# A gated-delta-rule recurrence: substitution in one piece ahead of the keys' taps, keys by row on ScalarE, two projections tied behind the feed-forward

## The chip, the core and the metric

The kernel runs on one core of a Trainium2 chip. The core has TensorE (PE in the profile, its weight loads PEld), VectorE (DVE), ScalarE (ACT), GpSimd (POOL) and SyncE (SP), which here only issues DMAs. Each engine has its own queue of instructions, worked through in order; they wait for each other through semaphores. The metric is the device time of one execution in microseconds (us), the median of the runs shown.

## The reference, cut to what matters

Two transformer layers over 2 sequences of 1024 tokens with 256 features, layernorm after every block, all in float32: attention with 32 heads of 8 (8 key heads), a feed-forward with silu gate and int8 weights, a gated delta rule with 16 heads of 128, and a feed-forward with signs as weights. The change lies in the third block:

```python
q = _silu(_dwconv_causal(x @ Wq, conv_q_w, conv_q_b))      # k and v likewise; 4 taps
alpha = _sigmoid(x @ Wa + ba); beta = _sigmoid(x @ Wb + bb)
def step(S, inp):                                          # over the tokens, one by one
    qt, kt, vt, at, bt = inp
    err = einsum('bhvk,bhk->bhv', S, kt) - vt
    S = at * S - bt * err[..., None] * kt[:, :, None, :]
    o = einsum('bhvk,bhk->bhv', S, qt)
    return (S, o)
o = layernorm(o) * ln_w + ln_b
out = (o * sigmoid(x @ Wg)) @ Wo
```

## The kernel before, in words

The first layer (attention in two passes, then its feed-forward) takes the time up to about 820 us. Its feed-forward is a generator (`before` in `delta_rule`, L147), so that the first steps of the delta rule run beside it.

The delta rule works in **steps** `i` = 0 to 31: four halves of 512 tokens (two for each sequence) times 8 slots of two heads (L37, L38). One step takes two heads through 512 tokens in four chunks of 128. A chunk is solved as a block (`recur`, L590): pr = v + M k (L618, L622), copied to prs on ACT (L625); pw = inverse times prs (L633), copied to wc on ACT (L636); pm = keys by row times wc (L645), from which DVE makes the next state M (L650, L652); po = output (L659, L660), copied on ACT (L663). Each needs the one before.

Around `recur` stand the helpers of other steps, which fill PE between these matmuls:

- `keys(i+4)` (L283) projects the keys (L891 to L893, three matmuls for each of two halves of the 256 features), convolves them (`conv`, L258), makes the decays `at` with a scan on DVE (L306), the triangle `lt` of keys against keys (L315, L316), and stores its 32x32 diagonal blocks to DRAM (L328). `conv` is one evacuation on ACT (L265), three taps on DVE (L272) under `tc.high_priority()`, in the second half of a sequence the ends carried over from the first (L278), and a silu on ACT (L279). For the first slot of such a half, `carry` (L249) computes these ends on POOL, with a scratch tile `part` that shares the tag "tmp", and so the two buffers, with the substitution's scratch tile `tmp`.
- `blocks(i)` (L338), once for two steps, inverts 16x16 triangles by forward substitution. It loads the stored blocks into `ll` (L345), copies the identity into a PSUM bank on ACT (L355), and does 15 times a product and a difference on DVE (L360, L363; 128x15 to 128x64 elements). Then ACT copies the result to `tt` (L365), one DMA stores it (L367), eight load it in another arrangement as `dt` (L373), and DVE transposes it into `dd` (L376).
- `levels(i)` (L379), once for two steps, builds the inverse of the whole 128x128 triangle from these blocks in several rounds of small matmuls. Its first (L387, 128 matmuls) reads `dd`, its second (L397) `n0` made on DVE (L389), and DVE transposes a second time (L401).
- `others(i+1)` (L494): projections of v and q (`pair`, L446), `key_rows` (L452: four transposes of the keys on PE, L458, then one DVE instruction over 128x512 that scales them by the last decay of their chunk, L460), the gate's projection (L483), `scores` (L465, L470, L471), `decayed` (L477).
- `finish` (L528) normalizes the outputs (o on POOL, DVE and ACT, L555, L558), transposes them (L564), applies the gate (ACT L567, DVE L568), and projects them (L891 to L893 with tile pf).

The **order of the work** has three sources. `Places` (L95) writes the helpers' pieces out by hand: a step has 120 units, each `yield` names the unit of the next piece (AT_BLOCKS = 44 and 52 and then 2.2 units for each substitution step, AT_LEVELS from 43 of the next step, AT_KEYS = 91). From step 0 on, `InLine.link` (L133) ties every matmul to the one written before it (`te.strict`, L772), so that PE's order is the written one. On the other engines a planner that simulates the time puts the ready instruction with the best priority next; priority is the order of writing, and `tc.high_priority()` moves an instruction ahead of all normal ones. `after(a, b)` (L895) ties the order of two instructions without a wait across engines.

Where the feed-forward ends: at i = -2 it is drained (L776), and the first `blocks` and `others(0)` are written; at i = -1 come `keys(3)`, the first `levels`, the opening of the late pools (L780), whose memory is that of the feed-forward, and `rest_of_first` (L516), which holds the decays of step 0 and the projections of v and q for step 1. PE's order is not yet written here. At i = 0 come `recur(0)` and `gate_of_first` (L523), whose weights wg lie in the late pools.

Of the kernel before, what the change touches and what calls it, by code (L numbers as in the profile page):

```python
# [11 lines left out]
F32 = mybir.dt.float32  # L12
# [3 lines left out]
AF = mybir.ActivationFunctionType  # L16
ALU = mybir.AluOpType
# [3 lines left out]
P = 128  # L21
# [9 lines left out]
SCALE = DK ** -0.5  # L31
# [3 lines left out]
HC = HT // P  # L35
Q = 4
BL = P // Q  # L37
SB = BL // 2  # L38
U = HP * HC
# [104 lines left out]
def delta_rule(  # L144
# [13 lines left out]
    nc = tc.nc  # L158
# [3 lines left out]
    early = open_pool(left, "dearly", "left", 2)  # L162
# [24 lines left out]
    def q4(t):  # L187
        return t.rearrange("p (c t) -> p c t", t=P)
# [12 lines left out]
    dt = cst.tile([P, 2 * U, BL], F32, name="dt", tag="dt")  # L201
    nc.gpsimd.memset(lo, 0.0)
    nc.gpsimd.memset(dt, 0.0)
    ib = load(a["c_ib"], [P, BL], "ib")
# [23 lines left out]

    st = [dict() for _ in range(B * 2 * NS)]
    state, lines, copied = [None] * NS, Places(te), []  # L230
    last = B * 2 * NS - 1

    def place(i):
# [24 lines left out]
    def conv(m, i, h, bufs, pp):  # L258

        hi, s = place(i)  # L260
        n, hd = "qkv".index(m), s * HP + h
        acc = half_tile(early if m == "k" else conv_pool, m, bufs)

        with tc.high_priority():
            nc.scalar.activation(  # L265
                acc, pp, AF.Identity, bias=cb[:, n, hd : hd + 1], scale=cw[:, n, hd, KS - 1 : KS]
            )
            if hi % 2 == 0:
                nc.scalar.copy(halos[:, n, hd, :], pp[:, HT - KS + 1 :])

            for d in range(1, KS):
                made = nc.vector.scalar_tensor_tensor(  # L272
                    acc[:, d:], pp[:, 0 : HT - d], cw[:, n, hd, KS - 1 - d : KS - d], acc[:, d:], ALU.mult, ALU.add
                )
        if hi % 2:
            if s == 0 and h == 0:
                carry(n)
            nc.vector.tensor_add(acc[:, 0 : KS - 1], acc[:, 0 : KS - 1], ends[:, n, hd, :])  # L278
        nc.scalar.activation(acc, acc, AF.Silu)  # L279
        st[i][m, h] = acc  # L280
        return made

    def keys(i, t0):  # L283

        hi, s = place(i)
        col = halves[hi]["col"]
        pps = [project("k", i, h) for h in range(HP)]
        if i < last:
            st[i + 1]["wk"] = weights("k", place(i + 1)[1])
        for h in range(HP):  # L290
            taps = conv("k", i, h, 10, pps[h])
        yield t0 + AT_DECAY - AT_KEYS
        lt = early.tile([P, U, P], F32, name="lt", tag="lt", bufs=5)
        st[i]["lt"] = lt
        nc.gpsimd.memset(lt[:, :, 0:1], 0.0)
        for h in range(HP):
            hd = s * HP + h
            dec = decay(hi, hd, 0, "da")
            d1 = early.tile([P, HC, P], F32, name="d1", tag="raw", bufs=RAW)
            nc.gpsimd.affine_select(  # L300
                d1, col[:, :, hd].unsqueeze(2).to_broadcast([P, HC, P]),
                pattern=[[0, HC], [1, P]], compare_op=ALU.is_equal, fill=0.0, base=0, channel_multiplier=-1,
            )
            e = half_tile(early, "at", 10)
            after(
                nc.vector.tensor_tensor_scan(e, dec, d1.rearrange("p c t -> p (c t)"), 0.0, ALU.mult, ALU.add), taps  # L306
            )
            st[i]["at", h] = e
        for h in range(HP):
            yield t0 + AT_TRIANGLE[h] - AT_KEYS  # L310
            e, k = st[i]["at", h], st[i]["k", h]
            pkk = bank(ps_m, "m", "pkk")
            for c in range(HC):
                t = slice(c * P, (c + 1) * P)
                te.link(nc.tensor.matmul(pkk[:, t], lhsT=k[:, t], rhs=k[:, t], start=True, stop=True))  # L315
            nc.vector.scalar_tensor_tensor(  # L316
                lt[:, h * HC : (h + 1) * HC, 1:P], q4(pkk)[:, :, 1:P], SCALE, q4(e)[:, :, 0 : P - 1],
                ALU.mult, ALU.mult,
            )
        yield t0 + AT_TRIANGLE[2] - AT_KEYS  # L320
        n = i % 2
        if n == 0:
            st[i]["d1"] = dram.tile([Q, 2 * U, BL, BL], F32, name="d1_", tag="d1_")
        else:
            st[i]["d1"] = st[i - 1]["d1"]
        for q in range(Q):
            r = slice(q * BL, (q + 1) * BL)
            nc.sync.dma_start(  # L328
                out=st[i]["d1"][q, n * U : (n + 1) * U].rearrange("u j t -> j u t"), in_=lt[r, :, r]
            )  # L330
# [7 lines left out]
    def blocks(i, psum):  # L338

        NB = Q * 2 * U  # L340
        ll, tt, dd = split_block(i)
        d1 = st[i]["d1"]
        for h in range(2):
            r = slice(h * SB, (h + 1) * SB)
            nc.sync.dma_start(  # L345
                out=ll[h * NB : (h + 1) * NB], in_=d1.rearrange("q u j t -> (q u) j t")[:, r, r]
            )
        nc.sync.dma_start(out=tt.rearrange("p c r -> p (c r)"), in_=a["c_idl"])
        for q in range(Q):
            nc.sync.dma_start(  # L350
                out=lo[q * BL : q * BL + SB, :, SB:BL], in_=d1[q, :, 0:SB, SB:BL].rearrange("u j t -> j u t")
            )
        yield AT_BLOCKS[1]
        wide = bank(*psum, "pi")[:, 0 : SB * SB].rearrange("p (c r) -> p c r", r=SB)
        nc.scalar.copy(wide, tt)  # L355
        for j in range(SB - 1):
            n, m = j + 1, SB - 1 - j
            tmp = early.tile([P, 64], F32, name="tmp", tag="tmp")
            tm = tmp[:, 0 : n * m].rearrange("p (c r) -> p c r", r=m)
            nc.vector.tensor_mul(  # L360
                tm, wide[:, 0:n, j : j + 1].to_broadcast([P, n, m]), ll[:, j : j + 1, j + 1 : SB].to_broadcast([P, n, m])
            )
            nc.vector.tensor_sub(wide[:, 0:n, j + 1 : SB], wide[:, 0:n, j + 1 : SB], tm)  # L363
            yield AT_BLOCKS[1] + BLOCK_STEP * (j + 1)
        nc.scalar.copy(tt, wide)  # L365
        d2_ = dram.tile([2, Q, 2 * U, SB, SB], F32, name="d2_", tag="d2_")
        nc.sync.dma_start(  # L367
            out=d2_.rearrange("h q u c r -> (h q u) (c r)"), in_=tt.rearrange("p c r -> p (c r)")
        )
        for q in range(Q):  # L370
            for h in range(2):
                o = q * BL + h * SB
                nc.sync.dma_start(  # L373
                    out=dt[o : o + SB, :, h * SB : (h + 1) * SB], in_=d2_[h, q].rearrange("u c r -> c u r")
                )
        nc.vector.transpose(dd, dt.rearrange("p u t -> p (u t)"))  # L376
        st[i]["dd"] = dd.rearrange("p (u t) -> p u t", t=BL)

    def levels(i, psum):  # L379

        dd = st[i]["dd"]
        quarter = [slice(q * BL, (q + 1) * BL) for q in range(Q)]
        p0 = bank(*psum, "p0").rearrange("p (u t) -> p u t", t=BL)
        with tc.high_priority():
# [1 line left out]
                for r in quarter:  # L386
                    te.link(nc.tensor.matmul(p0[r, v, :], lhsT=lo[r, v, :], rhs=dd[r, v, :], start=True, stop=True))  # L387
        n0 = early.tile([P, 2 * U, BL], F32, name="n0", tag="tt", bufs=1)
        nc.vector.scalar_tensor_tensor(  # L389
            n0, p0, -1.0, ib.unsqueeze(1).to_broadcast([P, 2 * U, BL]), ALU.mult, ALU.add  # L390
        )
        yield AT_LEVELS[1]
        px = bank(*psum, "px").rearrange("p (u t) -> p u t", t=BL)
        with tc.high_priority():
# [3 lines left out]
        nc.scalar.copy(X[0 : 3 * BL, :, 0:BL], px[0 : 3 * BL])  # L398
        nc.scalar.copy(X[quarter[1], :, BL : 2 * BL], px[quarter[1]])

        nc.vector.transpose(dd.rearrange("p u t -> p (u t)"), px.rearrange("p u t -> p (u t)"))  # L401
        for n in range(2):
            for r in quarter:
                (nc.gpsimd.tensor_copy if n else nc.scalar.copy)(
# [46 lines left out]

    def key_rows(i, h):  # L452

        k, e = st[i]["k", h], st[i]["at", h]
        pk = bank(ps_m, "m", "pk")
        for c in range(HC):
            t = slice(c * P, (c + 1) * P)
            te.link(nc.tensor.transpose(pk[:, t], k[:, t], ident))  # L458
        kc = conv_pool.tile([P, HC, P], F32, name="kc", tag="kc", bufs=4)
        nc.vector.scalar_tensor_tensor(  # L460
            kc, q4(pk), -SCALE, q4(e)[:, :, P - 1 : P].to_broadcast([P, HC, P]), ALU.mult, ALU.mult
        )
        st[i]["kc", h] = kc

    def scores(i, h):  # L465
# [11 lines left out]
    def decayed(i, h):  # L477

        q, k, gs = st[i]["q", h], st[i]["k", h], st[i]["dg"][h]
        nc.gpsimd.tensor_mul(q4(k)[:, :, 1:P], q4(k)[:, :, 1:P], q4(gs)[:, :, 0 : P - 1])  # L480
        nc.gpsimd.tensor_mul(q, q, gs)
# [34 lines left out]
    def rest_of_first():  # L516
        decays(0)
        for h in range(HP):
            decayed(0, h)
        for m in "vq":  # L520
            pair(m, 1)

# [244 lines left out]
    def drain(g):  # L767
        for _ in g:
            pass

    for i in range(-AHEAD, last + 1):
        te.strict = i >= 0  # L772
        t = i * UNIT
        if i == -2:
            drain(blocks(0, (ps_m, "m")))
            drain(before)  # L776
        if i == -1:
            drain(keys(3, 0))
            drain(levels(0, (ps_m, "m")))
            open_late()  # L780
# [770 lines left out]
```

## Time and profile before

| | us |
|---|---|
| median of 3 runs | 2143.49 (2139.96 to 2144.91) |
| the profiled execution | 2145.29 |
| its span, first to last instruction | 2143.6 |
| PE busy in the span | 1916.0 (89%) |
| DVE busy | 1598.0 (75%) |
| ACT busy | 1111.1 (52%) |
| POOL busy | 789.0 (37%) |
| mean granted TensorE clock | 0.962 |

Lines of the profile are read so: in a list of groups, "L460 DVE SCALAR_TENSOR_TENSOR kc<-pk,at 128x512 x64" is line 460, run on DVE, writing tile kc from pk and at, 64 times, followed by the busy us, the mean ns of one, and the idle time of the engine just before them with what ended it. In a list of waits, "PE p L387 <- DVE ll L376: 16.6, 8, 5.1" says that PE stood 16.6 us in all ahead of L387, 8 times, at most 5.1 us, until DVE's instruction of L376 had ended. Where a wait is for several things, the list names the last event it saw. In a timeline each line has start, length, engine, line, operation, tiles and shape, a count of merged neighbours, and in brackets the idle time before it. The tile `ll` holds the blocks, the solution `tt` and the transposed `dd`; the tile p stands for p0 to p4, and pi for the PSUM bank `wide` of the substitution.

### The profile page before, as it was taken

Reading aid. Unit: us, or ns where it says so; the run is one execution under the profiler, and the core shown is the slowest. Engines: PE = TensorE matmul, PEld = TensorE weight load, DVE = VectorE, ACT = ScalarE, POOL = GpSimd, SP = SyncE. Lnnn points to the kernel's source line nnn. Section 1 sums busy time; section 2 is a strip of 40 time slices with the busy share of each in tenths; the row PEclk is TensorE's granted clock in tenths of the full one; section 3 lists DMA queues with packets and bytes.
Section 4 is the critical chain, followed back from the end, with each engine's and each line's share of the span. In section 5 each row is a group of like instructions: output and inputs, shape, how many; then the busy total and the mean of one; then the engine's idle time right before and its main releaser. Section 6 shows DMA issues by size and latency. Waiting matters only on the chain.

```text
span 2143.6 us, 48759 instructions
## 1 busy us (share of the span) xinstructions
PE 1916.0 (89%) x18656; PEld 1518.2 (71%) x18656; DVE 1598.0 (75%) x3886; ACT 1111.1 (52%) x2285; POOL 789.0 (37%) x1273
## 2 busy tenths in 40 slices
PE   4889999999987886989999899998988998988896
PEld 2455555555555886878888788887878887877775
DVE  6756666877748984888779778778777878866676
ACT  2365566576753453554544555554555554554442
POOL 1343332422122333444454344444344444334330
PEclk8999999999999998999999999999999999999997
DMA  7544443432033323434334434344433434433010
GB/s 222 162 149 139 141 142 119 156 103 78 34 81 108 92 65 89 122 102 122 97 106 119 121 108 117 104 124 113 128 102 98 138 89 122 117 103 91 20 46 20
DMA packets 313514, 230.91 MB, mean 108 GB/s; under 512 B 139648, under 2 KB 278656, under 8 KB 313280
## 3 DMA queue, kind: packets, MB, share of 16 engines
q1 hardware_dynamic: 299472, 210.80, 33.9%
q10 hardware_dynamic: 9632, 10.76, 1.5%
q0 software_dynamic: 4176, 6.23, 1.2%
q8 instruction: 147, 2.41, 0.5%
q14 instruction: 87, 0.71, 0.1%
HBM read 172.95 MB, written 51.87 MB: 105 GB/s over the span
## 4 chain that ended last, share of the span: by engine, by line
PE 53%; DVE 19%; DMA 6%; ACT 3%; SPq 3%; issue 3%; POOL 1%; POOLq 0%; ACTq 0%; DVEq 0%
PE av L1232 4%; PE ps L1211 4%; PE pp L891 4%; PE pp L893 4%; PE pp L892 4%; DVE k L272 3%; PE ps L1159 3%; DVE q L272 3%; PE pkq L470 3%; PE pm L645 2%; DVE v L272 2%; PE pr L622 2%; PE po L660 2%; SPq L373 2%; PE po L659 2%
## 5 line engine op out<-in xcount | busy, mean ns | idle before, releaser
L1168 DVE TENSOR_REDUCE mx<-ps 128x4 f32<-128x1024 f32 (+1 forms) x320 | 344.3, 1112 | 131.7 <-PE ps L1159 91.5
L1215 ACT ACTIVATE es<-ps 128x512 f32<-128x512 f32 (+1 forms) x608 | 315.2, 578 | 133.6 <-PE ps L1211 125.3
L1211 PE MATMUL ps<-qT,kT 128*128 128x512 f32 (+3 forms) x768 | 220.7, 369 | 17.6 <-ACT es L1215 15.5
L1159 PE MATMUL ps<-kT,qT 128*128 128x512 f32 x576 | 201.3, 424 | 20.9 <-DVE mx L1168 15.9
L1211 PEld LDWEIGHTS ps<-qT,kT 128*128 128x128 f32 x768 | 131.3, 190 | 104.9 <-ACT es L1215 53.7
L272 DVE SCALAR_TENSOR_TENSOR k<-pp,cw,k 128x511 f32<-128x511 f32 (+2 forms) x192 | 138.7, 741 | 45.1 <-ACT k L265 24.2
L272 DVE SCALAR_TENSOR_TENSOR q<-pp,cw,q 128x511 f32<-128x511 f32 (+2 forms) x192 | 138.9, 740 | 33.9 <-ACT q L265 16.4
L1232 PE MATMUL av<-es,vaug 128*32 128x512 f32 (+3 forms) x1536 | 162.6, 502 | 0.0
L1159 PEld LDWEIGHTS ps<-kT,qT 128*128 128x128 f32 x576 | 101.5, 191 | 82.1 <-DVE mx L1168 49.0
L272 DVE SCALAR_TENSOR_TENSOR v<-pp,cw,v 128x511 f32<-128x511 f32 (+2 forms) x192 | 138.2, 740 | 11.1 <-ACT v L265 7.1
L571 POOL CAST yh<-y 128x512 fp32r<-128x512 f32 x62 | 38.0, 613 | 271.4 <-DVE y L568 237.4
L841 POOL TENSOR_TENSOR wfl<-wf,wfh 128x256 fp32r<-128x256 f32 x80 | 58.6, 736 | 207.9 <-ACT wfh L929 181.3
L1218 POOL TENSOR_SCALAR_AFFINE_SELECT es<-es 128x512 f32<-128x512 f32 x128 | 80.7, 639 | 146.4 <-ACT es L1215 146.1
L300 POOL TENSOR_SCALAR_AFFINE_SELECT d<-col 128x512 f32<-128x512 f32 x64 | 59.9, 954 | 143.9 <-DVE at L306 126.9
L480 POOL TENSOR_TENSOR k<-k,dg 128x508 f32<-128x508 f32 x64 | 81.3, 1271 | 76.8 <-PE pkq L470 55.9
L625 ACT COPY prs<-pr 128x256 f32<-128x256 f32 x128 | 47.6, 372 | 114.7 <-PE pr L622 95.7
L660 PE MATMUL po<-wc,at 128*128 128x128 f32 x512 | 100.4, 285 | 0.0
L663 ACT COPY o<-po 128x256 f32<-128x256 f32 x128 | 47.5, 371 | 100.5 <-PE po L660 99.9
L659 PE MATMUL po<-M,q 128*128 128x128 f32 x448 | 90.8, 286 | 0.0
L622 PE MATMUL pr<-M,k 128*128 128x128 f32 x448 | 81.2, 276 | 8.4 <-DVE M L650 5.9
L633 PEld LDWEIGHTS pw<-prs,lt 128*128 128x128 f32 x512 | 78.3, 194 | 13.4 <-ACT prs L625 2.1
L1232 PEld LDWEIGHTS av<-es,vaug 128*32 128x32 f32 x1536 | 39.2, 110 | 67.7 <-issue 53.0
(309 smaller groups left out, 5600.9 us busy)
## 6 DMA issues: line engine op xcount, KB each, us to landing
wk<-w1k SPq DMA_DIRECT2D x64, 256.0 KB
da<-dec SPq DMA_DIRECT2D x64, 256.0 KB
wv<-w1v SPq DMA_DIRECT2D x64, 256.0 KB
wq<-w1q SPq DMA_DIRECT2D x64, 256.0 KB
dg<-dec SPq DMA_DIRECT2D x64, 256.0 KB
wg<-w1g SPq DMA_DIRECT2D x64, 256.0 KB
wo<-w1o SPq DMA_DIRECT2D x64, 256.0 KB
ad<-avs ACTq DMA_DIRECT2D x32, 256.0 KB
```

What stands on the lines that cost most here:

```text
L272: made = nc.vector.scalar_tensor_tensor(acc[:, d:], pp[:, 0 : HT - d], cw[:, n, hd, KS - 1 - d : KS - d], acc[:, d:], ALU.mult, ALU.add)
L622: te.link(nc.tensor.matmul(pr[:, r], lhsT=st[i]["k", h][:, t], rhs=M[:, r], start=False, stop=True))
L659: te.link(nc.tensor.matmul(po[:, r], lhsT=st[i]["q", h][:, t], rhs=M[:, r], start=True, stop=False))
L660: te.link(nc.tensor.matmul(po[:, r], lhsT=st[i]["at", h][:, t], rhs=wc[:, r], start=(M is None), stop=True))
L891: te.link(nc.tensor.matmul(out, lhsT=lhi, rhs=rhi, start=k0, stop=False))
L892: te.link(nc.tensor.matmul(out, lhsT=lhi, rhs=rlo, start=False, stop=False))
L893: te.link(nc.tensor.matmul(out, lhsT=llo, rhs=rhi, start=False, stop=k1))
L1159: anchor["mm"] = te.link(nc.tensor.matmul(ps[:, j - j0, :].rearrange("p (g k) -> p g k", k=P), lhsT=q_, rhs=kT[:, :, j * P : (j + 1) * P], ...
L1168: nc.vector.tensor_reduce(mx[:, it, j0 // 2, :], ps[:, 0:n, :].rearrange("p j (g k) -> p g j k", k=P), AX.XY, ALU.max)
L1211: te.link(nc.tensor.matmul(ps[:, g - g0, :], lhsT=kT[:, g, jb * P : (jb + 1) * P], rhs=qT[:, i0 : i0 + w], start=True, stop=True,))
L1215: exps.append(nc.scalar.activation(es[:, g0 : g0 + n, 0:w], ps, AF.Exp, scale=D ** -0.5))
L1232: mm = te.link(nc.tensor.matmul(av[ROW * g : ROW * (g + 1), i0 - ih * 512 : 512], lhsT=vaugs[b][:, jb, kv, :], rhs=es[:, g, 0:w], start=(j ...
```

## The change

The diff, its core (nothing of it is left out but context):

```diff
     state, lines, copied = [None] * NS, Places(te), []
+    ended, solved = [], []
...
   conv, the taps:
                 made = nc.vector.scalar_tensor_tensor(
                     acc[:, d:], pp[:, 0 : HT - d], cw[:, n, hd, KS - 1 - d : KS - d], acc[:, d:], ALU.mult, ALU.add
                 )
+                if m == "k" and d == 1 and solved:
+                    after(made, solved[-1])
...
   keys, behind the scan:
             st[i]["at", h] = e
+            em = early.tile([P, HC], F32, name="em", tag="em", bufs=10)
+            nc.gpsimd.tensor_scalar(em, q4(e)[:, :, P - 1], -SCALE, None, ALU.mult)
+            st[i]["em", h] = em
...
   blocks:
-            nc.vector.tensor_mul(
-                tm, wide[:, 0:n, j : j + 1].to_broadcast([P, n, m]), ll[:, j : j + 1, j + 1 : SB].to_broadcast([P, n, m])
-            )
-            nc.vector.tensor_sub(wide[:, 0:n, j + 1 : SB], wide[:, 0:n, j + 1 : SB], tm)
+            with tc.high_priority():
+                nc.vector.tensor_mul(
+                    tm, wide[:, 0:n, j : j + 1].to_broadcast([P, n, m]),
+                    ll[:, j : j + 1, j + 1 : SB].to_broadcast([P, n, m]),
+                )
+                made = nc.vector.tensor_sub(wide[:, 0:n, j + 1 : SB], wide[:, 0:n, j + 1 : SB], tm)
             yield AT_BLOCKS[1] + BLOCK_STEP * (j + 1)
-        nc.scalar.copy(tt, wide)
+        solved.append(made)
+        with tc.high_priority():
+            nc.scalar.copy(tt, wide)
...
-        nc.vector.transpose(dd, dt.rearrange("p u t -> p (u t)"))
+        with tc.high_priority():
+            nc.vector.transpose(dd, dt.rearrange("p u t -> p (u t)"))
...
   levels: n0 (L389) and the second transposition (L401) likewise under tc.high_priority()
...
   key_rows:
-        k, e = st[i]["k", h], st[i]["at", h]
+        k, em = st[i]["k", h], st[i]["em", h]
...
-        nc.vector.scalar_tensor_tensor(
-            kc, q4(pk), -SCALE, q4(e)[:, :, P - 1 : P].to_broadcast([P, HC, P]), ALU.mult, ALU.mult
-        )
+        for c in range(HC):
+            nc.scalar.activation(kc[:, c, :], q4(pk)[:, c, :], AF.Copy, scale=em[:, c : c + 1])
...
   rest_of_first:
+        te.strict, te.last = True, ended[0]
         for m in "vq":
             pair(m, 1)
...
   the main loop, i == -2:
             drain(before)
+            ended.append(te.last)
```

In words. (1) The 30 instructions of the forward substitution, the copy of its result, both transpositions and n0 get high priority, and the first tap of the keys is ordered behind the last difference of the latest substitution written. (2) The keys by row are scaled on ACT, one instruction for each chunk of 128 tokens, with the decay as an operand by partition; that operand, `em`, is made by a small instruction on POOL behind the scan. (3) The projections of v and q of step 1 are tied behind the last matmul of the feed-forward, in the written order.

More of the change, by code (lines that the diff above doesn't have):

```diff
@@ L388, in levels @@
         n0 = early.tile([P, 2 * U, BL], F32, name="n0", tag="tt", bufs=1)
-        nc.vector.scalar_tensor_tensor(
-            n0, p0, -1.0, ib.unsqueeze(1).to_broadcast([P, 2 * U, BL]), ALU.mult, ALU.add
-        )
+        with tc.high_priority():
+            nc.vector.scalar_tensor_tensor(
+                n0, p0, -1.0, ib.unsqueeze(1).to_broadcast([P, 2 * U, BL]), ALU.mult, ALU.add
+            )
         yield AT_LEVELS[1]
@@ L399, in levels @@
         nc.scalar.copy(X[quarter[1], :, BL : 2 * BL], px[quarter[1]])
-        nc.vector.transpose(dd.rearrange("p u t -> p (u t)"), px.rearrange("p u t -> p (u t)"))
+        with tc.high_priority():
+            nc.vector.transpose(dd.rearrange("p u t -> p (u t)"), px.rearrange("p u t -> p (u t)"))
         for n in range(2):
@@ L459, in key_rows @@
         kc = conv_pool.tile([P, HC, P], F32, name="kc", tag="kc", bufs=4)
-        nc.vector.scalar_tensor_tensor(
-            kc, q4(pk), -SCALE, q4(e)[:, :, P - 1 : P].to_broadcast([P, HC, P]), ALU.mult, ALU.mult
-        )
+        for c in range(HC):
+            nc.scalar.activation(kc[:, c, :], q4(pk)[:, c, :], AF.Copy, scale=em[:, c : c + 1])
         st[i]["kc", h] = kc
```

## The prediction

> **What bounds the kernel now.** I read the page's busy shares first: PE is busy 89% of the span, DVE 75%, ACT 52%, POOL 37%, so PE is the engine to watch. Next came the table by stretches. From 874 us on the recurrence repeats every two steps (a "pair" below), and I cut it from one start of the levels' first matmul (L387) to the next. Columns: length, then busy us and count of PE, PEld, DVE, ACT and POOL, then the granted clock.
>
> ```profile
> 1104.50:1185.90 81.40, 71.93 (x892) 64.72 (x892) 66.04 (x196) 39.90 (x79) 35.16 (x58) 0.96 0.38 109
> 1339.10:1413.30 74.20, 69.79 (x888) 62.60 (x888) 59.49 (x159) 39.73 (x86) 33.82 (x58) 1.00 0.40 112
> 1725.30:1807.10 81.80, 72.29 (x894) 65.07 (x894) 66.15 (x196) 39.87 (x79) 35.13 (x58) 0.96 0.39 108
> ```
>
> The work is nearly equal (70 to 72 us of PE), the length is not: 74.2 against 81.8 us. The difference is waiting, so the third view is PE's waits from 874 to 1957 us (total, times, longest).
>
> ```profile
> PE p L387 <- DVE ll L376: 16.6, 8, 5.1
> PE pt L564 <- DVE y L568: 15.9, 17, 1.0
> PE p L387 <- DVE ln L861: 11.8, 2, 5.9
> PE pkk L315 <- ACT k L279: 10.0, 2, 5.0
> PE pp L891 <- DVE v L272: 9.8, 12, 2.0
> ```
>
> L387 waits 16.6 + 11.8 = 28.4 us for the inverted blocks, transposed at L376; the name L861 is what DVE did meanwhile. The timeline of one pair shows why they are late.
>
> ```profile
> 1072.16 0.16 DVE L360 TENSOR_TENSOR tmp<-pi,ll 128x15 f32<-128x15 f32 x1
> ...
> 1096.07 0.17 DVE L363 TENSOR_TENSOR pi<-pi,tmp 128x15 f32<-128x15 f32 x1
> ...
> 1103.70 0.71 DVE L376 STREAM_TRANSPOSE ll<-dt 128x512 f32<-128x512 f32 x1 [0.35 <-DMA dt<-d__12429]
> ```
>
> Thirty tiny steps last 24 us because other work runs between them; copy, store, eight loads and transposition take 7.5 us more. The 10.0 us of L315 are two waits of 5.0, at the first pair of slot 0 in each second half. POOL's timeline names their cause.
>
> ```profile
> 1016.41 0.25 POOL L255 TENSOR_TENSOR part<-halos,cw 128x16 f32<-128x16 f32 x1 [0.81 <-DVE pi L363]
> ```
>
> carry's tile `part` shares the two buffers of tag "tmp" with the substitution, so the keys' ends, their silu and the matmul stand behind the slow chain. Last, PE where the feed-forward ends:
>
> ```profile
> 819.48 0.50 PE L1411 MATMUL po<-w_down,fhl 128*128 128x256 f32 x2 [0.31 <-POOL fhl L841]
> 833.74 0.76 PE L891 MATMUL pp<-x2h,wg 128*128 128x512 f32 x1 [13.76 <-DMA wg<-w1g]
> ```
>
> PE stands 13.76 us for the gate's weights, loaded only after the last layernorm (its end 826.10, x stored by 826.5, wg issued at 827.54, 6.06 us of transfer in the chain of waits).
>
> **The change, part by part.**
>
> Substitution first. Where nothing interrupts it, six steps took 1.53 us (1080.10 to 1081.63), 0.25 each; thirty are 7.6 us. Its block is loaded by issues ending at 1068.5; the store's landing (1096.81 to 1098.56, 1.75 us) gives an estimate of 1070.2. Taps of q and a state update go ahead, so it ends about 1080 instead of 1096.2. The 7.5 us behind it put the transposition at 1088; PE asks at 1103.7. The slowest tail in the trace, 1872.1 to 1885.8 (13.7 us), still fits. I take away all 28.4 us. The cover is 16 us; without it the old wait stands.
>
> Carry. With "tmp" free early, POOL, idle 5.98 us ahead of L300 at 1013.54, can run it before the scans. If it stays behind L300 it ends about 1 us earlier. Bounds -10.0 and -2; I take -8, nearer the row where POOL is idle.
>
> Fewer interruptions. Steps of 0.1 to 0.2 us also stand between v's taps, for which the second projection of q waits 9.8 us. Between 0 and -5; I take -2.
>
> Order. The piece stands ahead of all that was between its steps, the keys' taps too: in this pair they began at 1082.19, behind its new end, so cost 0. A state update (L652) can be caught: it ended at 1071.59 and its matmul came at 1072.23, a slack of 0.6 us. Two steps, 0.5 us, for each of 16 pieces give +8; bounds 0 and the rival below. On SP the store and eight loads (1.75 us of waiting, 3.74 of issue) now stand earlier, before loads of weights that have most of a step left; ACT's high copy of 0.37 us waits for a chain that nothing breaks any more. Both 0, in the same +8 if not.
>
> Keys by row. 64 DVE instructions of 0.678 us go (-43.4 us of DVE). 256 pieces of 128x128 come on ACT, an operation the trace does not show. Bounds: the 128x256 copy without operands by partition, 0.372, and L555 at 128x128 with two, 0.488. I take 0.40: L265 (0.779) against the exponential (0.599, 128x512) puts one such operand at 0.09. Back to back L555 goes every 0.39, so less one operand 0.30: four take 1.3 us, 83 us in all, and ACT rises from 1111 to 1194 us, 56%. The cover: between prs and its reader stand 12 matmuls (3 us), between wc and its reader 1 us; PE waits 3.7 us for ACT in the whole stretch. I charge +2 (0 to +10). The gain: at 1069.80 this instruction held back y (L568), for which L564 then waited 1.01 us; 0.6 us in up to 14 pairs is -8, the free place may go to another instruction, so -4. The new `em` is 0.22 us on POOL (as L866), 64 of it, in its idle 63%, but it waits for the scan in order; L300 waited there too; 0.
>
> Tied pairs. v and q of step 1 ran between 748 and 768 us, filling the feed-forward. There DVE is full (38.90 of 40 us, and 49.86 of 50 before). They take 12 taps x 0.74 = 8.9 us of DVE and 24 matmuls of about 0.25 = 6 us of PE along, so the feed-forward ends 6 to 10 us earlier; with the block's steps no longer spread and kc gone (1.4 us) I take 8. In PE's hole of 13.76 us the pairs cost nothing. But their taps are of high priority and the layernorm is not: it sets when wg is issued. It gave way to 0.1 us steps before; to 0.74 us taps it gives way more. Between 0 and +19 (8.9 of taps, 7.6 of substitution, 2 of evictions), I take +4: the chain has some 20 steps, and half of the taps come after it. Net -4, bounds -10 and +11.
>
> Clock. Eleven stretches between 952 and 1891 us, 68 us in all, ran at 0.50 with PE busy 54.3, at most 27 us lost. The thirteen full pairs sum to 1012.4; thirteen times the mean of the four with least wait (74.9) is 973.4. Of the 39.0 between, 34.7 are waits named above (28.4 + 10.0, less 3.7 in the four themselves). 4.3 are left; I take -4.
>
> Sum: -28.4 - 8 - 2 + 8 + 2 - 4 - 4 - 4 = -40.4. The profiled execution took 2145.29 us, 1.7 more than its span, and lies 1.8 above the median of 2143.49. 2145.3 - 40.4 gives **2105**.
>
> **The rivals.** (1) The clock. The 3.4 us ahead of each of the eleven stretches held 0 to 1.78 us of busy PE. If waiting alone halves the clock and PE is the bound behind it, all 27 us return: 2105 - 23 = 2082. Against it stand the 4.3 us above. The Trainium skill, page "TensorE: Matmul & The Clock Gate", Part 1, says that the clock halves after about one idle window of 3.4 us and comes back after a busy one. The trace agrees on the length of the steps (3.4 and 6.8 us), not on idle: 1.78 busy was enough to fall.
>
> (2) Given back: what was second becomes first. M, y and POOL's normalized o (5.5 us today) wait in the same places; if half of the gain goes there, or the layernorm of the tied pairs is fully delayed, 2126. For it: DVE is 80% busy in these pairs.
>
> (3) Slower. The first substitution step is queued on DVE the moment its load should have landed. If it is queued ahead of q's taps (1066.91) and the block lands at 1070.2, DVE stands 3.3 us in every piece with taps, y and M behind it: 16 x 3.3 = 53, 2158. It decides at 40.4 / 16 = 2.5 us of DVE idle before L360 in each pair. Against it: that wait is 3.9 us in all 240 today, and q's taps are written earlier.
>
> (4) It does not do what it says: the priority leaves the steps interleaved, the ties only order them. Then -5, about 2140.
>
> **How the numbers follow.** Forecast 0.52 (its own range 2090 to 2122), clock 0.12, given back 0.16, slower 0.12, no effect 0.08. A measurement of this kernel tells about 0.2% (4 us) from no change. The range goes from the clock's case to the edge of no effect, 2080 to 2140. Faster 0.52 + 0.12 + 0.16 + 0.03 = 0.83; same 0.05; slower 0.12.
>
> **What would show it.** Right: pairs of 74 to 76 us throughout, L387 without waits, the thirty steps within 8 to 10 us, L315's 5.0 us gone, fewer 0.50 stretches, PE's hole filled by wv and wq and at its start some 8 us earlier. Wrong: idle DVE before L360, more wait of L622 for M or of L633 and L645 for ACT, the last layernorm drawn out past 10 us, L387 still waiting.

## The result and the profile after

| | before | after |
|---|---|---|
| median, us | 2142.47 (4 runs, 2139.96 to 2144.91) | 2128.70 (4 runs, 2125.71 to 2130.01) |
| the profiled execution, us | 2145.29 | 2129.30 |
| its span, us | 2143.6 | 2127.6 |
| ACT / DVE busy, us | 1111.1 / 1598.0 | 1166.7 / 1570.9 |

The ratio is 0.9934, 95% interval 0.9917 to 0.9951: faster by 14 us, where 40 were forecast. The time lies in the range given, near the rival "given back" (2126).

The table by stretches of the changed kernel, each stretch from one start of the levels' first matmul to the next (columns as before: length, busy us and count of PE, PEld, DVE, ACT, POOL, then granted clock):

```profile
1099.10:1178.40 79.30, 72.06 (x893) 64.44 (x893) 63.04 (x192) 42.91 (x94) 34.64 (x60) 0.96 0.39 110
1338.90:1414.60 75.70, 70.90 (x889) 63.52 (x888) 57.40 (x154) 42.95 (x102) 34.56 (x62) 0.98 0.40 110
1717.90:1796.00 78.10, 72.26 (x901) 64.55 (x903) 63.21 (x196) 43.55 (x97) 34.49 (x60) 0.96 0.40 111
```

The pairs that took 81 us take 78 to 79, not 74 to 76, and the good pair (74.2) became 75.7; the longest is now another, 81.3 us (1257.6 to 1338.9), where it took 75.6. PE's waits from 864 to 1960 us (total, times, longest) show that there is waiting left, but under other names:

```profile
PE pr L636 <- DVE M L664: 16.4, 6, 3.6
PE pr L636 <- DVE M L666: 14.5, 5, 3.9
PE pp L906 <- DVE v L273: 11.2, 11, 2.5
PE pkk L322 <- DVE lt L323: 8.5, 3, 3.4
PE pt L578 <- DVE y L582: 7.3, 19, 1.7
PE pp L906 <- DVE k L273: 5.7, 9, 1.3
PE pt L578 <- ACT o L569: 4.6, 5, 1.0
```

The levels (28.4 us before) and the keys' silu behind carry (10.0) are gone from the list. At its head stands now the state update M with 30.9 us, where it had 8.5. VectorE's timeline of the pair that the prediction followed shows why (line numbers are those of the changed kernel: L368 and L372 the two halves of a substitution step, L388 the first transposition, L664 and L666 the state update):

```profile
1066.14 0.17 DVE L368 TENSOR_TENSOR tmp<-pi,ll 128x15 f32<-128x15 f32 x1
...
1077.14 0.18 DVE L372 TENSOR_TENSOR pi<-pi,tmp 128x15 f32<-128x15 f32 x1
...
1088.00 0.71 DVE L388 STREAM_TRANSPOSE ll<-dt 128x512 f32<-128x512 f32 x1 [2.10 <-DMA dt<-d__12517]
...
1090.79 0.68 DVE L323 SCALAR_TENSOR_TENSOR lt<-pkk,at 128x508 f32<-128x508 f32 x1
1091.39 0.48 DVE L664 COPY M<-pm 128x128 f32<-128x128 f32 x2
```

The thirty steps now take 11.2 us instead of 24, and the transposition comes at 1088.0, 11 us before the levels want it (1099.1). But it was put into VectorE's queue at a place where its loads had not landed: the engine stands 2.10 us, and behind it stand v's taps, the triangle `lt` and the copy that makes M. PE, whose order is written out, waits for that M (timeline of PE):

```profile
1086.41 0.67 PE L659 MATMUL pm<-wc,kc 128*128 128x128 f32 x4
...
1091.72 0.49 PE L636 MATMUL pr<-M,k 128*128 128x128 f32 x2 [3.20 <-DVE M L664]
```

pm, all that M needs, is done about 1087.1, 4.3 us before the copy begins. SP's queue shows where the landing loses time. Its timeline (start, length of the issues, number), first before, then after:

```profile
1096.81 0.33 SPq L367 DMA_DIRECT2D d__12429<-ll  x1
...
1098.56 3.74 SPq L373 DMA_DIRECT2D dt<-d__12429  x8
```

```profile
1076.45 0.87 SPq L222 DMA_DIRECT2D wk<-w1k  x2
1077.42 0.42 SPq L213 DMA_DIRECT2D dg<-dec  x1
1078.03 0.33 SPq L378 DMA_DIRECT2D d__12517<-ll  x1
1081.67 4.90 SPq L384 DMA_DIRECT2D dt<-d__12517  x8
```

The store of the block now stands right behind three loads of 256 KB, the first of them issued 1.6 us before it. From its issue to the first load of `dt` pass 3.6 us, before 1.75, and the eight issues take 4.9 instead of 3.7. It is the nearness of the loads that goes with the delay: in e1 below the same three are issued 3.3 to 2.1 us ahead of the store, and twelve such stores take 2.0 to 2.3 us; in the changed kernel the twelve take 3.5 to 4.0.

**An account of the recurrence.** From the levels of the second pair to those of the last I summed PE's idle time (gaps) and the time that PE was busy while the granted clock was 0.50; half of that counts as lost. Length less gaps less this loss (the remainder below) is 967 to 971 us in all fourteen kernels of this study, so the account closes.

| kernel | ratio to before (95%) | length | gaps | lost at 0.50 |
|---|---|---|---|---|
| before | 1 | 1083.2 | 88.8 | 27.3 |
| after | 0.9934 (0.9917 to 0.9951) | 1068.6 | 71.3 | 30.4 |
| e1 substitution alone | 0.9929 (0.9912 to 0.9946) | 1071.7 | 81.8 | 21.7 |
| e2 keys by row alone | 0.9879 (0.9859 to 0.9899) | 1059.7 | 66.4 | 23.4 |
| e3 ties alone | 1.0025 (1.0010 to 1.0040) | 1081.0 | 88.3 | 25.3 |
| e4 after, late transposition | 0.9827 (0.9804 to 0.9849) | 1046.2 | 62.7 | 14.0 |
| e5 after, no ties | 0.9921 (0.9904 to 0.9938) | 1068.6 | 72.0 | 27.4 |
| e6 e4, no ties | 0.9813 (0.9795 to 0.9830) | 1046.7 | 61.0 | 15.5 |
| e7 after, wk behind dt | 0.9868 (0.9855 to 0.9880) | 1057.9 | 69.8 | 16.9 |
| e8 e6, M ahead of v's taps | 0.9911 (0.9890 to 0.9932) | 1061.9 | 73.1 | 19.2 |
| e9 e1, late transposition | 0.9938 (0.9923 to 0.9953) | 1073.1 | 89.8 | 13.2 |
| e10 e2, carry's own buffer | 0.9866 (0.9845 to 0.9887) | 1060.1 | 69.8 | 22.1 |
| e11 e6, keys' taps not tied | 0.9879 (0.9861 to 0.9898) | 1063.5 | 71.6 | 22.0 |
| e12 e10, late transposition | 0.9885 (0.9868 to 0.9902) | 1056.5 | 66.7 | 20.4 |

Each ratio is to runs of the kernel before on the same chip (its medians there lay between 2142 and 2151 us, so the ratios are what compares). The start of the stretch moves by several us from one profiled execution to the next (the attention ended between 660.3 and 676.7), which is why single spans are not compared.

### The profile page after: what moved, and what is told of

Its sections match the earlier page's. It is cut to its first block, busy times and chain, and to the rows that moved or that the text cites. A ratio compares the mean times of both kernels' runs of the same rounds, so it can differ in the third digit from the quotient of the medians.

```text
span 2127.6 us, 48944 instructions
## 1 busy us (share of the span) xinstructions
PE 1920.9 (90%) x18656; PEld 1521.2 (71%) x18656; DVE 1570.9 (74%) x3822; ACT 1166.7 (55%) x2541; POOL 808.8 (38%) x1337
## 4 chain that ended last, share of the span: by engine, by line
PE 56%; DVE 13%; DMA 7%; ACT 4%; issue 3%; SPq 3%; POOL 1%; DVEq 0%; POOLq 0%; ACTq 0%
PE pp L906 5%; PE pp L907 5%; PE pp L908 5%; PE ps L1226 4%; PE av L1247 4%; PE ps L1174 3%; DVE q L273 3%; PE pkq L483 3%; DVE v L273 2%; SPq L384 2%; PE pr L636 2%; PE pm L659 2%; PE ph L1401 2%; PE pw L647 2%; PE po L674 2%
## 5 line engine op out<-in xcount | busy, mean ns | idle before, releaser
L1226 PE MATMUL ps<-qT,kT 128*128 128x512 f32 (+3 forms) x768 | 221.4, 370 | 17.8 <-ACT es L1230 16.0
L1233 POOL TENSOR_SCALAR_AFFINE_SELECT es<-es 128x512 f32<-128x512 f32 x128 | 80.4, 636 | 145.2 <-ACT es L1230 144.9
L636 PE MATMUL pr<-M,k 128*128 128x128 f32 x448 | 87.2, 291 | 30.8 <-DVE M L664 16.4
L493 POOL TENSOR_TENSOR k<-k,dg 128x508 f32<-128x508 f32 x64 | 81.3, 1270 | 83.3 <-PE pkq L483 50.6
L314 POOL TENSOR_SCALAR em<-at 128x4 f32<-128x4 f32 x64 | 41.1, 642 | 181.8 <-DVE at L309 179.4
L636 PEld LDWEIGHTS pr<-M,k 128*128 128x128 f32 x448 | 75.1, 209 | 34.1 <-DVE M L664 15.7
L944 ACT CAST wfh<-wf 128x256 fp32r<-128x256 f32 x80 | 32.3, 406 | 99.6 <-DMA wf<-in_w1k 27.0
```

The costliest lines, as they stand in the source:

```text
L636: te.link(nc.tensor.matmul(pr[:, r], lhsT=st[i]["k", h][:, t], rhs=M[:, r], start=False, stop=True))
L1226: te.link(nc.tensor.matmul(ps[:, g - g0, :], lhsT=kT[:, g, jb * P : (jb + 1) * P], rhs=qT[:, i0 : i0 + w], start=True, stop=True,))
```

## The experiments

**Each part alone: e1_sub, e2_rows, e3_ties.** Each takes two of the three parts out of the changed kernel again.

```diff
 e1_sub, against the changed kernel:
-            em = early.tile([P, HC], F32, name="em", tag="em", bufs=10)
...
-        for c in range(HC):
-            nc.scalar.activation(kc[:, c, :], q4(pk)[:, c, :], AF.Copy, scale=em[:, c : c + 1])
+        nc.vector.scalar_tensor_tensor(
+            kc, q4(pk), -SCALE, q4(e)[:, :, P - 1 : P].to_broadcast([P, HC, P]), ALU.mult, ALU.mult
+        )
...
-        te.strict, te.last = True, ended[0]
 e2_rows, against the changed kernel:
-                if m == "k" and d == 1 and solved:
-                    after(made, solved[-1])
...
-            with tc.high_priority():
...
-        te.strict, te.last = True, ended[0]
 e3_ties, against the kernel before:
+        te.strict, te.last = True, ended[0]
...
+            ended.append(te.last)
```

> The substitution in one piece alone, without the keys by row on ScalarE and without the ties. Theory (the early transposition stands in VectorE's queue until its loads land, and the state update behind it is late): about 10 us faster than before, near 2132; no wait of the levels' first matmul, but 20 us or more of wait of pr for M. Rival (what was given back comes from the keys by row: POOL's em behind the scan and ScalarE's small pieces): some 30 us faster, near 2112, and waits of pr for M below 10 us.

0.9929, some 15 us: nearer the theory's time (10) than the rival's (30), but without the theory's mechanism, for M waited only 7.5 us. The longest of PE's waits of e1:

```profile
PE pp L902 <- DVE k L273: 31.5, 13, 3.4
```

The levels never wait. But the keys' taps are ordered behind the piece, and the piece takes 13.3 us here, with kc's instruction (0.68 us) and others still between its steps. So the next projection waits 31.5 us for the banks that the keys' taps have not yet read. That wait was not in either expectation.

> The keys by row on ScalarE alone, all else as before. Theory: within 4 us of before, about 2140, because VectorE's 43 us are off the path. Rival: 10 us slower or more, 2152 and up, with new waits of PE for ScalarE (prs, wc) or for POOL's normalized o.

0.9879, some 26 us, the most of any part, which neither expectation had. PE's waits of e2:

```profile
PE pkk L319 <- DVE lt L320: 9.5, 3, 3.5
PE pkk L319 <- ACT k L279: 9.1, 2, 4.6
...
PE pt L567 <- DVE y L571: 4.9, 16, 0.5
PE p L391 <- DVE ll L380: 4.7, 3, 2.5
```

The levels' wait fell from 28.4 to about 5 us, with no priority changed, and that of y from 15.9 to 4.9. The instruction that left VectorE stood between the substitution's steps: they took 24 us and now 20 in the pair followed. Carry's waits (9.1) stayed. Idle time of VectorE ahead of the transposition does not tell a kernel's time by itself: it is 34.1 us in e2 and 17.5 in the kernel before, against 24.9 in the changed kernel. It matters what stands behind it: M waits 30.9 us in the changed kernel and 8.1 in e2.

> The tie of two projections behind the feed-forward alone. Theory: 4 us faster, about 2138, the gate's weights arriving some 3 us earlier and the recurrence behind that unchanged. Rival: no change, because the layernorm gives back all that the feed-forward wins.

1.0025: slower. The feed-forward's last matmul comes 1.5 us earlier after the end of attention, but the last layernorm ends 13.7 us behind it (6.1 before). VectorE's timeline of e3 at that place, where L865, L863 and L864 are the layernorm's chain:

```profile
833.41 0.15 DVE L865 SCALAR_TENSOR_TENSOR ln<-ln 128x2 f32<-128x2 f32 x1
...
833.61 1.39 DVE L273 SCALAR_TENSOR_TENSOR q<-pp,cw,q 128x511 f32<-128x511 f32 x2
834.92 0.15 DVE L863 TENSOR_TENSOR ln<-ln 128x2 f32<-128x2 f32 x1
```

Between links of 0.15 us stand taps of 0.74. The gate's matmul starts 5.6 us later relative to the attention.

**The transposition out of the way: e4_turn_late, e6_late_no_ties.** The transposition is written at the start of the levels and ordered behind the state update written last (`moved` lists the instructions that make M); e6 also drops the tie of v and q.

```diff
     def levels(i, psum):
         dd = st[i]["dd"]
+        with tc.high_priority():
+            turned = nc.vector.transpose(dd, dt.rearrange("p u t -> p (u t)"))
+        if moved:
+            after(turned, moved[-1])
```

> The changed kernel with one move: the first transposition of the blocks is written at the start of the levels and tied behind the state update of the step's first chunk. Theory: the wait of pr for M falls from 31 us to below 12 us, the levels still don't wait, and the time falls by 15 to 22 us to about 2110. Rival (the state update is late because of the taps of v ahead of it, not because of the transposition): the waits stay above 25 us and the time within 4 us of the changed kernel, 2125 to 2132.

0.9827, some 23 us below the changed kernel on one scale of ratios, as much as the theory hoped for, though M's waits did not fall below 12. VectorE's timeline of e4:

```profile
1095.83 0.48 DVE L667 COPY M<-pm 128x128 f32<-128x128 f32 x2
1096.22 0.70 DVE L393 STREAM_TRANSPOSE ll<-dt 128x512 f32<-128x512 f32 x1
```

No idle time in brackets: ahead of all sixteen transpositions VectorE now stands 0.7 us, in the changed kernel 24.9. M's waits fell from 30.9 to 19.3 and the levels still do not wait. The account tells more: of the 22.4 us that the recurrence is shorter, gaps are 8.6 and the clock is 16.4 (30.4 to 14.0; the remainder moved 2.6 the other way). The rows by stretch show it, first of the changed kernel (a wait and what follows it), then of e4:

```profile
1088.50:1091.70 3.20, 0.03 (x1) 0.00 (x0) 3.20 (x10) 0.00 (x0) 0.57 (x3) 1.00 0.96 262
1093.40:1096.80 3.40, 3.40 (x9) 2.66 (x10) 2.54 (x11) 1.32 (x3) 3.04 (x7) 0.50 0.33 72
```

```profile
1092.90:1096.30 3.40, 1.46 (x13) 1.22 (x13) 3.40 (x10) 0.67 (x2) 1.97 (x9) 1.00 0.70 155
1096.30:1099.70 3.40, 2.08 (x11) 1.47 (x11) 3.40 (x11) 1.98 (x5) 2.98 (x7) 1.00 0.89 277
```

After 3.2 us in which PE did nothing, 3.4 us ran at 0.50. Two shorter waits with work between them left the clock at 1.00. The Trainium skill, page "TensorE: Matmul & The Clock Gate", section "HAM oscillation — how this bites in real kernels", counts half of the throttled time as the cost that comes on top of the waits. The trace agrees: with half of the busy time at 0.50 taken off, the fourteen remainders lie within 4.2 us of each other; with the gaps alone taken off, they spread over 14.0 us.

> The changed kernel with the first transposition tied behind the state update, and without the tie of the two projections. Theory: 2101 to 2107, as with the tie; if the tie costs what it cost alone (5 us), 2100. Rival: 2110 or more.

0.9813, the best ratio of the study; its interval overlaps e4's. M waits 19.9 us. No gain of the ties is to be seen on top of e4.

**The ties out of the changed kernel: e5_no_ties.**

```diff
-        te.strict, te.last = True, ended[0]
```

> The changed kernel without the tie of the two projections. Theory (the feed-forward wins about as much by the tie as the last layernorm loses to the taps): within 4 us of the changed kernel, 2125 to 2132, with the last layernorm 6 to 7 us behind the feed-forward's last matmul instead of 11. Rival: the tie carries a part of the gain, and the time rises to 2134 or more.

0.9921 against 0.9934, intervals overlap. Without the tie the feed-forward ends 5.5 us later after the attention (150.7 against 145.2), and the layernorm behind it takes 6.1 us instead of 11.0. From the end of attention to the gate's first matmul it is 164.2 us without the tie, 163.2 with it, 167.5 before.

**The wait shortened instead: e7_wk_behind.** VectorE's order is as in the changed kernel. The keys' weights are loaded behind the eight loads of `dt` (`spread` lists these).

```diff
+            if m == "k" and spread:
+                after(made, spread[-1])
```

> The changed kernel, VectorE's order untouched; the loads of the keys' weights are ordered behind the eight loads that feed the transposition, so that its wait gets shorter without moving it. Theory (the transposition stands in the queue for its loads): VectorE's idle time ahead of it falls from 24.9 us to below 8, the wait of pr for M from 31 to about 12, the time to 2108 to 2118. Rival (the state update is late by its place behind the taps of v and the triangle): its wait stays above 25 us and the time above 2124.

0.9868. The wait shrank, but less than expected: the decays' loads (dg, 256 KB each) still go ahead of the store, and thirteen stores take 2.7 to 3.0 us to their first load. VectorE's line in e7, and PE's:

```profile
1090.18 0.71 DVE L390 STREAM_TRANSPOSE ll<-dt 128x512 f32<-128x512 f32 x1 [1.55 <-DMA dt<-d__12517]
```

```profile
1093.91 0.49 PE L638 MATMUL pr<-M,k 128*128 128x128 f32 x2 [2.65 <-DVE M L666]
```

The transpositions stand 17.8 us in all instead of 24.9, M waits 25.9 instead of 30.9. Gaps fell by only 1.5 us, the loss at 0.50 by 13.5 (the remainder grew by 4.3): nine stretches of mostly 3.4 us are left of fourteen, of which seven had 6.8. Between 2.5 and 3 us of wait the clock went both ways: this one of 2.65 was followed by 3.4 us at 0.50 (from 1095.8), one of 2.55 at 1325 by none. The length of a wait alone does not decide. In each of the fourteen traces the granted clock changes only at multiples of one step of 3.41 us, and what goes with a fall is how little PE worked within the step that ends there. Four waits of 2.65 us in e1, all ahead of L902, show it: two lie within one step, with 0.76 us of work left in it, and 0.50 follows (waits ending at 1009.2 and 1084.8 us); two lie across two steps, with 1.80 us of work or more in each, and the clock stays at 1.00 (1622.4 and 1700.4). e7 shows the same stall by another way than e4.

**M ahead of everything: e8_update_first.** In e6, the convolution of v's second head is also written later (at unit 21 of the step), and its taps are ordered behind the state update.

```diff
+                if m == "v" and h == 1 and d == 1 and moved:
+                    after(made, moved[-1])
```

> The kernel with the late transposition and without ties, and in addition the taps of v of the second head written and tied behind the state update of the first chunk. Theory: the wait of pr for M falls from 17 us to below 8, and the time by 5 to 10 us to about 2097. Rival: the projections' PSUM banks are held longer and the second projection waits for them instead, so that the time stays at 2101 or more.

0.9911, worse than e6: the rival. M waits only 3.0 us, but PE's list of e8 has a new head:

```profile
PE pp L921 <- DVE v L274: 41.9, 18, 4.5
```

e6 waits 18.9 us there. What waits longest is only moved, from M to the banks of the projections.

**The parts again, without the stall: e9_sub_late, e10_rows_carry, e11_no_key_tie, e12_rows_carry_late.** e9 is e1 with the late transposition. e10 is e2 with one edit, e11 is e6 without the order of the keys' tap, e12 is e10 with the late transposition.

```diff
 e10, in carry:
-            part = early.tile([P, H, KS - 1], F32, name="part", tag="tmp")
+            part = early.tile([P, H, KS - 1], F32, name="part", tag="part", bufs=1)
 e11, in conv:
-                if m == "k" and d == 1 and solved:
-                    after(made, solved[-1])
```

> The substitution part alone, without the keys by row on ScalarE and without the ties (as e1_sub), but with the first transposition written at the start of the levels and ordered behind the last state update (as e4_turn_late). It asks what the block's new place is worth by itself once nothing on VectorE stands and waits for its loads. Theory: the gains of the substitution part and of the keys by row are mostly the same gain, since both take away the same 28.4 us of waits of the levels. Then this kernel lands at -0.9 to -1.5% (ratio 0.985 to 0.991), near the keys by row alone (0.9879), and the two together (e6_late_no_ties, 0.9813) give less than their sum. In e1_sub the transposition stood idle for only 9.4 us, so at most 0.45% is to be had from moving it there. Rival: the keys' taps tied behind the substitution are the price (31.5 us of waits of v's projections for PSUM banks in e1_sub); then the late transposition changes nothing and the ratio stays at 0.992 to 0.994.

0.9938, as e1: the rival. The 31.5 us for the keys' taps stayed, and y took 18.8:

```profile
PE pp L905 <- DVE k L273: 31.5, 13, 3.4
```

So the substitution part needs the room that the keys by row leave on VectorE: with it the same order costs 5.7 us, without it 31.5. The theory that the two parts are mostly one gain does not hold either: e9 and e2 alone bring 13 and 26 us, and e6, which has both, brings 40.

> The keys by row on ScalarE alone (e2_rows), with one more change: carry's scratch tile gets a buffer of its own instead of sharing the substitution's two. Theory: what e2_rows leaves of the old waits is 9.1 us at the keys of slot 0 in the second halves (the carry) and 6.2 us of the levels. A buffer of its own takes the 9.1 us away: about -0.4% against e2_rows' 0.9879, so 0.982 to 0.986, as good as the substitution in one piece with the late transposition. Rival: POOL's order puts carry no earlier, since its other inputs or its place in POOL's queue decide; then the ratio stays at 0.986 to 0.990 and the two waits of about 4.5 us stay.

0.9866, as e2 (0.9879): the rival's ratio, but not its reason. Carry's 9.1 us are gone, but 15.2 us appeared ahead of the outputs' transposes (L567; e2 had 7.0). VectorE's and PE's timelines of e10:

```profile
1090.21 0.71 DVE L380 STREAM_TRANSPOSE ll<-dt 128x512 f32<-128x512 f32 x1 [3.33 <-DMA dt<-d__12517]
...
1091.48 0.16 DVE L551 SCALAR_TENSOR_TENSOR om<-om 128x8 f32<-128x8 f32 x1
```

```profile
1092.22 0.90 PE L567 MATMUL pt<-ident,o 128*128 128x128 f32 x3 [3.45 <-ACT o L558]
```

It is the same stall with another victim: the normalizing scalars (L551) stand behind the transposition, ACT waits for them, PE for ACT.

> As e6_late_no_ties, without the order that puts the first tap of the keys behind the last difference of the substitution: the substitution keeps its high priority. Theory: with the block's load on time the substitution goes ahead of the keys' taps by itself or is cut by at most six taps of 0.74 us (4.4 us), and the levels, asked for 15 us later, do not see it: same as e6_late_no_ties within 0.3% (0.978 to 0.985). Rival 1: the tie costs, since the keys' taps hold PSUM banks while the chain runs (5.7 us of waits for k in the changed kernel): better by up to 0.3%, 0.978. Rival 2: the tie is what holds the piece together, and without it the waits of the levels come back: 0.985 to 0.99.

0.9879 against e6's 0.9813: the second rival's size, but not its mechanism. Without the order of the keys' tap the substitution is cut up again (20 us a pair), high priority or not. The levels' first matmul hardly waits (3.8 us); carry and the others do:

```profile
PE pkk L320 <- ACT k L280: 9.1, 2, 4.5
PE pt L578 <- ACT o L569: 9.0, 3, 3.5
```

> The keys by row on ScalarE, carry's own scratch buffer (as e10_rows_carry), and the first transposition written at the start of the levels and ordered behind the last state update; nothing of the substitution part and no ties. In e10_rows_carry the 9.1 us of carry's waits went, but 15.2 us appeared ahead of the transposed outputs (L567), each time right behind a transposition that stood 2.9 to 3.6 us in VectorE's queue for its loads, with the output's last normalizing scalars behind it. Theory: this stall is the one thing that gives gains back, here as in the changed kernel. With the transposition later its idle time falls from 37 us to under 12, the 15.2 us to under 6, and the ratio to 0.977 to 0.983, as good as e6_late_no_ties. Rival: the chain ends so late here (the substitution still ends 7 us later than in one piece) that the transposition has to be waited for anyway; its idle time stays above 25 us or becomes a wait of the levels, and the ratio stays at 0.985 to 0.989.

0.9885: the rival. VectorE still stands 31.0 us ahead of the transpositions in all, 3.72 in the pair followed (until 1101.13).

Being behind the last M does not help when the loads land still later. In e4 and e6, where the piece ends early, the loads have landed by M's turn (0.7 us of idle time each).

## Why the prediction was wrong

The direction and most of the list of mechanisms were right; the sum was 26 us too large. Its step that failed is **"Order ... Both 0, in the same +8 if not"**: 8 us for all that is caught behind the moved work. Measured in its place: M +22.4 us of waits, the keys' taps +5.7 (forecast 0), `lt` +4.0, ACT's o +4.6, which is 36.7. The sum looked for what the thirty steps would catch; what stood in the way was the transposition behind them, early in VectorE's queue and waiting for its loads.

- **Substitution, -28.4.** Right in place and size: the levels wait no more. That the transposition came at 1088.0, where 1088 was forecast, is luck: the steps ended at 1077.3 instead of 1080, and the way from there took 10.7 us instead of 8. The slack of 11 us behind it (16 forecast) was real, but I read it only as cover for the levels. A transposition that is early in an engine's queue and late in its data is a stall for everything behind it, and here the next things in the queue were v's taps and M. I asked what the thirty steps could catch (0.5 us each pair) and not what the one instruction with a DMA behind it could. e4 leaves 0.7 of the 24.9 us of idle time and is 23 us faster. Not all of M's wait is that stall: 19.3 us are left in e4, with v's taps ahead of M, and e8 takes those only at the price of v's waits.
- **SP at 0.** Wrong: the prediction had the store ahead of the loads of weights, but the keys' weights are issued 1.6 us before it, and it took 3.6 us instead of 1.75. e7 changes only such an order of loads and gives back about 14 us.
- **Carry, -8.** It gained all of its 10.0 us of waits. e10 shows that its worth depends on what is next: with the keys by row (e10 against e2) it bought nothing that the intervals show.
- **Fewer interruptions, -2.** Not seen: 10.0 us of v's waits became 11.2.
- **Keys by row, +2 and -4.** The ACT side was near: 0.376 us for a piece (0.40 estimated), ACT up by 56 us (83 forecast); the 4.6 us of waits for o go with the stall, e4 has none. The gain was mis-sized by far. Alone the part brings about 26 us, because each 0.68 us stood in the way of the substitution and of y, and because the levels' chain, which I had given wholly to the first part, gets 23 us shorter waits from it. The parts alone bring 15 and 26 us, together 14, because the stall takes the rest: with the transposition late, the two together bring 37 (e4) and 40 (e6), about their sum. Both shorten the levels' wait, but each also helps the other: the keys by row take the keys' taps from 31.5 to 5.7 us.
- **Tied pairs, net -4** (-8 for the feed-forward, +4 for the layernorm). The measured -8.5 and +4.9 fit, but for the wrong reason: without the tie (e5) the way to the gate's matmul is already 3.2 us shorter than before, with it 4.3. The tie only trades one for the other, and alone it is slower.
- **Clock, -4.** It went up by 3.1. I had divided the pairs' surplus into named waits and a rest, as if a wait had only its own price. Most waits of 2.5 us and more, those that leave little work in one 3.41 us step, cost a second time in half clock; the changed kernel has fourteen such stretches in the account's span, before had eleven, e4 six. Rival 1's 27 us are the right size of what is there to gain (27.3), of which e9 got 14 and e4 13.
- **The rivals.** "Given back" (2126) is near to what happened, with M at the head as it named, but y fell (15.9 to 7.3 us), and ACT's o came for POOL's. It did not name the transposition that waits for its loads, and its half of the gain was not worked out from a wait, so that its time fits is luck. The slower case's point (VectorE idle ahead of the first step) did not occur: 0.5 us in all.

Not settled: why the projections' waits for v grow to 20.6 us in e4 as M's fall, beyond what e8 shows of that exchange, and how the remaining 19 us of M could go without it.

## What to carry to other kernels

Moving an instruction up moves its wait up too: before giving priority to one that reads a DMA, compare the landing with the place in the queue, and look at what stands behind it on that engine. If a change has several parts, try each alone as well as together; here the smallest one (an instruction taken off the full engine) brought more than the whole change. Count a wait of some 3 us on TensorE twice, once for itself and once for the half clock that mostly follows.

## What the runs showed of the hardware

- The granted clock follows the work within one step, not the length of a wait. Its changes lie on one grid of 3.41 us in each of the fourteen traces. From 864 to 1960 us it fell behind 151 steps at full clock, in which PE had been busy for at most 1.88 us; behind 4117 others it stayed, and in these PE had been busy for at least 1.57 us. Between 1.57 and 1.88 us both occurred.

- What makes a small POOL instruction long here is what VectorE runs beside it. `em`, 128x4 elements, where I had put 0.22 us, took 1.05 as the first of a pair and 0.23 as the second (64 times, mean 0.64). All 32 long ones run beside VectorE's second scan (`at`) and end 0.02 to 0.04 us after it; none of the 32 short ones runs beside a scan. In the kernel before it was L300: 1.4 to 1.6 us for the 24 that ran beside a scan, 0.63 to 0.68 for the other 40. Behind `em` the same instruction (L303) takes 0.64 on average, so that POOL's busy time rose by 19.8 us (789.0 to 808.8) and not by the 41.1 of `em`.

- A store followed by loads of it, from its issue to the first load, from 870 us on: 1.7 to 1.95 us where no 256 KB load is issued in the 3.3 us ahead (nine stores of the kernel before), 2.7 to 3.0 with one load 0.7 to 0.8 us ahead (thirteen in e7), 3.5 to 4.0 with three, the first 1.6 to 1.7 us ahead (twelve in the changed kernel), and 2.0 to 2.3 with the same three, the first 3.3 us ahead (twelve in e1).
